# A four-layer graph attention stack on one core: attention logits computed by matmuls of their own, ahead of the values, and the third layer's sums copied out by ScalarE and scaled on GpSimd

## The chip, the cores and the metric

The kernel runs on one core of a Trainium2 chip. Its time is the device time of one execution in microseconds (us). The kernel before was run three times: 3017.86, 3018.09 and 3025.92 us, median 3018.09. The engines are named as in the profile: PE is TensorE (PEld its weight loads), ACT is ScalarE, DVE is VectorE, POOL is GpSimd, SP is SyncE, which issues most DMAs.

## The reference

There are 16 graphs of 1024 nodes with 256 features, and an adjacency matrix for each. Four attention layers follow each other; each normalises x, applies relu, attends, and adds the result to x. Layers 0, 1 and 2 have four heads of 64 columns, layer 3 has one head of 256. In layers 0 and 1 it is, cut to what matters:

```python
h = jnp.maximum(_layernorm(x, axis=-1), 0.0)
v = (h @ W).reshape(B, N, H, HD)                      # values
s = einsum('bnhd,hd->bhn', v, a1); d = einsum('bmhd,hd->bhm', v, a2)   # logits' two halves
e = leaky_relu(s[:, :, :, None] + d[:, :, None, :], 0.2)
e = where(adj == 0, -inf, e)
x = x + einsum('bhnm,bhmd->bhnd', softmax(e), v)
```

Layer 3 is the same with one head. Layer 2 has one pair of vectors for each edge type and, after the attention, adds a bias, takes relu, adds v, and normalises each head's 64 columns with gamma and beta. As adj holds only 0 and 1, only the first edge type occurs in the fast path that is measured here.

So s and d are vectors, one number for each node and head, and linear in h: they can be had as h times (W a), without v.

## The kernel before, in words

Nodes of a graph lie in 8 blocks of 128. A *unit* is one layer of one graph, so there are 64. For a unit with four heads there are 32 *tiles*, one for each head h and source block j; a tile is 128 x 1024 numerators. A tile passes three engines: `weigh` (ACT, lines 991 to 996) makes r = relu(scale * row + bias) in one of two PSUM buffers r; `cover` (DVE, line 1009) adds a constant, multiplies with the mask and writes p to one of 13 buffers in SBUF; `gather` (PE, line 1075) issues 16 matmuls of 65 columns that add p times the values, and the sum of p in column 65, into one of two PSUM banks `po`. This works without a maximum per row because the exponential of a leaky relu splits into products of factors `fac` that depend on one node only, and into a row, kept as `rows`, that depends on the other. All tiles of layers 0 to 2 together are 16 x 3 x 32 = 1536. Layer 3 has work of its own, `last_layer` and `last_sums` (lines 1178 and 1193), which is fitted in between.

What goes before a unit is `prepare` (line 801): bn_stats on DVE, nine small operations `rs` on POOL, and then for each of four *pairs* of blocks: two normalised blocks `hn` on POOL, four transposes on PE, relu to `hT` (`normal`, line 750), and for each block of the pair `project` (line 777): four matmuls of the turned block with the weights `wa`. The weights of each head have two further columns, W times the two attention vectors, made once at the start by `weights` (line 640). So one projection gives, per head, 64 values, s and d: 4 x 66 = 264 columns, in layer 3 258, copied from PSUM to `v`. When all eight blocks are there, DVE takes the maximum of s and d (`wide`, line 861), PE and DVE turn and spread it, DVE and ACT make the factors, and the row goes through DRAM into `rows`. `others` (line 890) makes the remaining factors, and then either POOL multiplies the values by a factor (`flatten`, layers 0 and 1) or writes 1 into the values' column for the sum (layers 2 and 3).

What comes after a tile's sums is `evacuate` (line 1108): in layers 0 and 1 a copy of the PSUM bank to `att`, in layer 2 on DVE a reciprocal of the sums and a multiply. `finish` (line 1128) then works on both halves of a head: in layers 0 and 1 a reciprocal on DVE and a multiply on POOL, in layer 2 the bias and normalisation, and at last the addition to x, all mostly on POOL. For the last two heads of the last unit of the tiles, `main[-1]`, DVE does what POOL does elsewhere.

The order on every engine is fixed when the program is built. A planner (`Plan`, line 417) keeps a clock for each engine with costs (`cost`, line 437) and picks, again and again, the job that can begin first; among jobs that can begin within `NEAR` = 60 ns of the first it takes the one with the earliest due time (`until`). Every engine then runs its list in order. Units of two graphs alternate (`LANES` = 2). Copies marked `EITHER` may go to ACT or DVE; with `DVE_MORE` = 1e9 they go to ACT. There are two PSUM banks `pp` for everything else than r and po (`BANKS` = 2), and three `hT` buffers (`PAIRS` = 3): a pair's buffer is free when all that read it have been issued. All engine operations are issued through one helper, so that nearly every line of the profile shows L487, and tiles are told apart by their names.

## Time and profile before

| | |
|---|---|
| median of three runs | 3018.09 us |
| profiled execution, its own time | 3014.36 us |
| its span, first to last instruction | 3012.4 us |
| granted TensorE clock, mean | 0.976 |
| busy: PE, PEld, DVE, ACT, POOL | 2694.6, 2262.8, 2650.3, 2414.9, 1571.0 us |
| instructions | 130240 |

The rows of the profile name an operation by its output and inputs, its shape and its number; the page gives, for each, the busy time, the mean of one, and the idle time of the engine just before it. The busy time of an engine is the union of its operations, and an operation's duration can reach into the next one's. The waits are listed as "who waited for whom: us in total, times, longest". A matmul in the code is two instructions in the profile, each with a weight load of its own.

### The profile page before, as it was taken

The numbers are of one execution on the slowest core, as the hardware profiler recorded it, in microseconds if no ns is written. First come the engines' busy times: TensorE is split into PE (matmuls) and PEld (weight loads), VectorE is DVE, ScalarE is ACT, GpSimd is POOL, SyncE is SP. The second block draws the span as 40 slices with busy tenths as digits, with TensorE's granted clock in tenths as the row PEclk, the third lists the DMA queues.
The fourth block names the chain that finished last, engine by engine and source line by source line (L and its number), as shares of the span: only waits on it lengthen the run. The fifth ranks groups of instructions, "written<-read, shape, count | busy, mean of one in ns | idle before, by whom it ended". The sixth has DMA issues, their size and how long they took to land.

```text
span 3012.4 us, 130240 instructions
## 1 busy us (share of the span) xinstructions
PE 2694.6 (89%) x58915; PEld 2262.8 (75%) x58915; DVE 2650.3 (88%) x4065; ACT 2414.9 (80%) x3201; POOL 1571.0 (52%) x2263
## 2 busy tenths in 40 slices
PE   5888889999998989999898998989989899999867
PEld 4777777787776778778787786878778778887745
DVE  5889899899978989898998989989898998999963
ACT  5898888888878788888879788897888879878641
POOL 3445682754736447375463745637375464463630
PEclk8999999999999999999999999999999999999978
DMA  7323211323122131413113141321413213111100
GB/s 139 73 59 73 64 36 55 70 65 83 52 52 74 64 68 55 90 44 82 52 63 76 38 96 38 78 59 61 83 42 80 57 62 73 49 48 49 39 12 28
DMA packets 144292, 186.91 MB, mean 62 GB/s; under 512 B 80760, under 2 KB 116336, under 8 KB 142704
## 3 DMA queue, kind: packets, MB, share of 16 engines
q1 hardware_dynamic: 141680, 161.71, 18.5%
q0 software_dynamic: 2048, 16.78, 5.7%
q8 instruction: 464, 7.60, 1.0%
q14 instruction: 100, 0.82, 0.1%
HBM read 194.38 MB, written 34.40 MB: 76 GB/s over the span
## 4 chain that ended last, share of the span: by engine, by line
PE 35%; DVE 29%; ACT 21%; POOL 7%; issue 5%; DMA 1%; SPq 0%; ACTq 0%; POOLq 0%; DVEq 0%
DVE p L487 19%; PE pp L487 19%; PE po L487 16%; ACT r L487 15%; DVE st L487 3%; POOL att L487 2%; ACT seen L487 2%; DVE att L487 2%; ACT att L487 1%; DVE s L487 1%; DVE c L487 1%; POOL rs L487 1%; POOL hn L487 1%; ACT v L487 1%; ACT hT L487 1%
## 5 line engine op out<-in xcount | busy, mean ns | idle before, releaser
L487 ACT ACTIVATE r<-rows,fac 128x1024 f32<-128x1024 f32 (+1 forms) x1552 | 1766.0, 1148 | 363.3 <-DVE p L487 339.3
L487 PEld LDWEIGHTS po<-v,p 128*64 128x64 f32 x49216 | 1598.1, 140 | 332.4 <-DVE p L487 150.6
L487 PE MATMUL po<-v,p 128*64 128x65 f32 x49216 | 1665.0, 225 | 202.0 <-DVE p L487 128.7
L487 DVE SCALAR_TENSOR_TENSOR p<-r,mask 128x1024 f32<-128x1024 f32 x1024 | 1220.5, 1217 | 112.2 <-ACT r L487 86.8
L487 DVE SCALAR_TENSOR_TENSOR p<-r,fac,mask 128x1024 f32<-128x1024 f32 (+1 forms) x768 | 817.9, 1098 | 88.3 <-ACT r L487 71.0
L487 PE MATMUL pp<-wa,hT 128*64 128x264 f32 (+1 forms) x4056 | 518.3, 391 | 13.6 <-ACT hT L487 10.2
L487 POOL TENSOR_TENSOR att<-att,inv 128x512 f32<-128x512 f32 x128 | 133.9, 1046 | 744.6 <-DVE inv L487 628.3
L487 PE MATMUL pp<-v_one,p 128*64 128x257 f32 x3584 | 430.7, 383 | 2.7 <-DVE p L487 1.8
L487 PEld LDWEIGHTS pp<-wa,hT 128*64 128x64 f32 x4056 | 269.3, 138 | 138.9 <-ACT hT L487 16.5
L487 PEld LDWEIGHTS pp<-v_one,p 128*64 128x64 f32 x3584 | 267.2, 138 | 95.2 <-DVE p L487 9.0
L487 POOL TENSOR_SCALAR hn<-x_cur,rs 128x256 f32<-128x256 f32 x512 | 281.6, 562 | 36.4 <-PE pp L487 22.3
L487 PE MATMUL pp<-ident,hn 128*128 128x128 f32 x1020 | 178.8, 295 | 63.5 <-POOL hn L487 51.8
L487 POOL TENSOR_TENSOR x_cur<-att,x_cur 128x512 f32<-128x512 f32 x190 | 226.3, 1191 | 14.9
L487 ACT ACTIVATE r<-rows_one,fac 128x512 f32<-128x512 f32 x240 | 183.4, 778 | 19.3 <-DVE p L487 9.9
L487 PEld LDWEIGHTS pp<-ident,hn 128*128 128x128 f32 x1020 | 108.4, 143 | 120.3 <-POOL hn L487 91.9
L487 DVE BATCH_NORM_STATS2 st<-x_cur 128x6 f32<-128x256 f32 x512 | 180.8, 410 | 11.9 <-DMA x_cur<-in_x_dram 10.2
L487 ACT ACTIVATE hT<-pp 128x512 f32<-128x512 f32 x255 | 147.7, 594 | 39.3 <-PE pp L487 37.9
L487 ACT COPY v<-pp 128x264 f32<-128x264 f32 (+1 forms) x395 | 146.3, 383 | 21.1 <-PE pp L487 18.9
L487 POOL TENSOR_TENSOR v<-v,fac 128x512 f32<-128x512 f32 x128 | 136.1, 1088 | 47.3 <-ACT fac L487 47.3
L487 POOL TENSOR_TENSOR att<-att,s 128x512 f32<-128x512 f32 x124 | 133.1, 1074 | 10.0
L487 ACT ACTIVATE seen<-mask 128x1024 bf16<-128x1024 fp8e4 x128 | 134.6, 1052 | 0.4
L487 POOL TENSOR_TENSOR rs<-st 128x8 f32<-128x8 f32 x192 | 37.9, 211 | 153.9 <-DVE st L487 138.8
(91 smaller groups left out, 1616.3 us busy)
## 6 DMA issues: line engine op xcount, KB each, us to landing
rows<-line SPq DMA_DIRECT2D x191, 512.0 KB
x_cur<-in_x_dram SPq DMA_DIRECT2D x32, 512.0 KB
near<-in_adj_dram POOLq DMA_DIRECT2D x64, 256.0 KB, 8.1
out_dram<-y SPq DMA_DIRECT2D x128, 128.0 KB
rows_one<-line SPq DMA_DIRECT2D x15, 512.0 KB
mask<-near SPq DMA_TRANSPOSE x64
wa<-in_L_gnn_W_dram SPq DMA_DIRECT2D x6, 128.0 KB
line<-row SPq DMA_DIRECT2D x48, 16.0 KB
```

Of the source, the lines that this page charges most:

```text
L487: r = call(*a, **k)
```

## The change

It does four things.

1. Logits. A new job `logits` for each pair of blocks: eight matmuls of the turned blocks with the two further columns of all heads (8 columns, in layer 3 two), into a `pp` bank, and one copy to a new small tile `sd`. `project` now leaves these columns out: 256 columns instead of 264 or 258, and rows of `v` have 65 columns for each head instead of 66. `prepare` goes on to the maximum as soon as `sd` is complete. A pair's `hT` buffer is now read by three jobs.
2. Due times. Logits take the due time that projections had; projections are due `BEHIND` = 20 tiles later.
3. Values. `flatten`, or the writing of ones, waits for the values itself; `fac` loses an unused quarter, and its numbering moves by one; `st`, `rs` and `c` have three buffers instead of two. The planner's cost of a matmul with at most 16 output columns is 30 ns.
4. Evacuation. In layer 2, all units but the last of the tiles are treated as layers 0 and 1 are: a copy of the sums by ACT, then a reciprocal for the head on DVE and the multiply on POOL in `finish`.

```diff
+BEHIND = 20
...
-            return swap + max(59.0, size(out) * 0.833 + 3.0), PE_LATE
+            return swap + (30.0 if size(out) <= 16 else max(59.0, size(out) * 0.833 + 3.0)), PE_LATE
...
+        add(u.until, logits(e), plan.now)
         for i in range(2):
-            add(u.until, project(e, i), plan.now)
+            add(u.until + BEHIND, project(e, i), plan.now)
+
+    def logits(e):
+
+        u = e.u
+        yield "PE", lambda: u.layer in folded and free_for(u) and max(folded[u.layer], free_for(u))
+        pd, left = bank_for(u)
+        pd = pd[:, : 2 * 2 * u.n].rearrange("p (i h c) -> p i h c", i=2, c=2)
+        for i in range(2):
+            for k in range(KC):
+                for c in range(0, P, P // 2):
+                    at = i * P + c
+                    pe.matmul(
+                        pd[c : c + P // 2, i],
+                        e.hT[:, k, at : at + P // 2],
+                        wa[u.layer][:, k, :, u.w :],
+                        start=(k == 0 and i == 0),
+                        stop=(k == KC - 1),
+                        skip_group_check=True,
+                    )
+        e.left -= 1
+        e.read = plan.now
+        yield EITHER, None
+        either_copy(u.sd[:, 2 * e.pair : 2 * e.pair + 2], pd)
+        left()
+        u.begun += 2
+        u.known = plan.now
...
-                    wa[u.layer][:, k, :, :].rearrange("p h e -> p (h e)"),
+                    wa[u.layer][:, k, :, : u.w],
...
-        st = small.tile([P, NB, 2, 3], F32, name="st", bufs=2)
+        st = small.tile([P, NB, 2, 3], F32, name="st", bufs=3)
...
-            e.u, e.pair, e.turned, e.left = u, pair, False, 2
+            e.u, e.pair, e.turned, e.left = u, pair, False, 3
...
-        yield "DVE", lambda: not u.left and u.there
-        s, d = (v[:, :, :, w + c].rearrange("p b h -> p h b") for c in range(2))
+        yield "DVE", lambda: u.begun == NB and u.known
+        s, d = (u.sd[:, :, :, c].rearrange("p b h -> p h b") for c in range(2))
...
-            yield "POOL", None
+            act.activation(u.fac[:, 0:2], arg[:, 1:3], AF.Exp)
+            if not u.shared:
+                yield "POOL", None
+                pool.tensor_scalar(u.fac[:, 2], u.fac[:, 1], -1.0, 0.0, ALU.mult, ALU.add)
+            u.ready = plan.now
+            yield "POOL", lambda: not u.left and u.there
...
+    by_copy = lambda u: u is not main[-1]
...
-        yield EITHER if u.shared else "DVE", lambda: finishing[0] < ATTS or (u, h) in taking
+        yield EITHER if by_copy(u) else "DVE", lambda: finishing[0] < ATTS or (u, h) in taking
...
-        if u.shared:
+        if by_copy(u):
             either_copy(att[:, q, :], po)
...
-        if u.shared:
+        if by_copy(u):
             yield "DVE", None
             dve.reciprocal(u.inv[:, h, :], total)
             yield name, None
             eng.tensor_mul(att, att, wide(u.inv[:, h, :]))
```

More of the change, by code (lines that the diff above doesn't have):

```diff
@@ L554, in fast_path @@
     WIDTH = [F // n + 2 for n in HEADS]
-    VW = max(n * w for n, w in zip(HEADS, WIDTH))
+    VW = max(n * (w - 1) for n, w in zip(HEADS, WIDTH))
     MAXN = max(HEADS)
@@ L773, in normal @@
         left()
+        add(u.until, logits(e), plan.now)
         for i in range(2):
-            add(u.until, project(e, i), plan.now)
+            add(u.until + BEHIND, project(e, i), plan.now)
[23 more added lines that the diff above has]
+        u.known = plan.now
     def project(e, i: int):
         u = e.u
-        width = u.n * (u.w + 2)
         yield "PE", lambda: u.layer in folded and free_for(u) and max(folded[u.layer], free_for(u))
         pv, left = bank_for(u)
+        pv = pv[:, :F].rearrange("p (h e) -> p h e", h=u.n)
         for k in range(KC):
@@ L786, in project @@
                 pe.matmul(
-                    pv[c : c + P // 2, :width],
+                    pv[c : c + P // 2, :],
                     e.hT[:, k, at : at + P // 2],
-                    wa[u.layer][:, k, :, :].rearrange("p h e -> p (h e)"),
+                    wa[u.layer][:, k, :, : u.w],
                     start=(k == 0),
@@ L795, in project @@
         yield EITHER, None
-        either_copy(u.v[:, 2 * e.pair + i, :width], pv[:, :width])
+        either_copy(u.v[:, 2 * e.pair + i, : u.n * (u.w + 1)].rearrange("p (h e) -> p h e", h=u.n)[:, :, : u.w], pv)
         left()
@@ L804, in prepare @@
         slope = SLOPE[layer]
-        width = n * (w + 2)
+        width = n * (w + 1)
         yield "DVE", lambda: (
@@ L816, in prepare @@
         v = u.v[:, :, :width].rearrange("p b (h e) -> p b h e", h=n)
+        u.sd = small.tile([P, NB, n, 2], F32, name=f"sd{n}", bufs=3)
         plan.now = max(plan.now, u.g.here)
         xt = u.g.x
-        st = small.tile([P, NB, 2, 3], F32, name="st", bufs=2)
+        st = small.tile([P, NB, 2, 3], F32, name="st", bufs=3)
         for i in range(NB):
@@ L824, in prepare @@
         yield "POOL", None
-        rs = small.tile([P, 6, NB], F32, name="rs", bufs=2)
+        rs = small.tile([P, 6, NB], F32, name="rs", bufs=3)
         m0, m1, q0, q1 = st[:, :, 0, 1], st[:, :, 1, 1], st[:, :, 0, 2], st[:, :, 1, 2]
@@ L860, in prepare @@
         mx = mine[:, 1, : 2 * n].rearrange("p (c h) -> p c h", c=2)
-        dve.tensor_reduce(mx, v[:, :, :, w : w + 2].rearrange("p b h c -> p c h b"), AX.X, ALU.max)
+        dve.tensor_reduce(mx, u.sd.rearrange("p b h c -> p c h b"), AX.X, ALU.max)
         yield "PE", free_bank
@@ L874, in prepare @@
         yield "DVE", None
-        c = small.tile([P, 7, MAXN], F32, name="c", bufs=2)
+        c = small.tile([P, 7, MAXN], F32, name="c", bufs=3)
         S, D, t, c1, c2, b1, b3 = (c[:, i, :n] for i in range(7))
@@ L887, in prepare @@
         dve.scalar_tensor_tensor(arg[:, 0], s, 1.0 - slope, wide(b1), ALU.mult, ALU.add)
-        u.fac = small.tile([P, 4, n, NB], F32, name=f"fac{n}", bufs=3)
+        u.fac = small.tile([P, 3, n, NB], F32, name=f"fac{n}", bufs=3)
         def others():
@@ L901, in others @@
             yield "ACT", None
-            act.activation(u.fac[:, 1:3], arg[:, 1:3], AF.Exp)
-            yield "POOL", None
+            act.activation(u.fac[:, 0:2], arg[:, 1:3], AF.Exp)
[4 more added lines that the diff above has]
+            yield "POOL", lambda: not u.left and u.there
             if u.shared:
@@ L907, in others @@
                 pool.memset(v[:, :, :, w], 1.0)
-                pool.tensor_scalar(u.fac[:, 3], u.fac[:, 2], -1.0, 0.0, ALU.mult, ALU.add)
                 u.flat = plan.now
-            u.ready = plan.now
         add(u.until, others(), plan.now)
@@ L959, in flatten @@
     def flatten(u: "Unit", v: bass.AP):
-        flat = u.fac[:, 2].rearrange("p h b -> p b h")
+        flat = u.fac[:, 1].rearrange("p h b -> p b h")
         for b in range(0, NB, 2):
@@ L993, in weigh @@
         r, k = wide_bank()
-        base = -1.0 if u.shared else u.fac[:, 3, h, j : j + 1]
-        act.activation(r, u.row[h][0], AF.Relu, bias=base, scale=u.fac[:, 1, h, j : j + 1])
+        base = -1.0 if u.shared else u.fac[:, 2, h, j : j + 1]
+        act.activation(r, u.row[h][0], AF.Relu, bias=base, scale=u.fac[:, 0, h, j : j + 1])
         weighed.append((u, None, h, j, r, k, plan.now))
@@ L1004, in weigh_some @@
         for k in range(MANY):
-            scale = u.fac[:, 1, 0, j + k : j + k + 1]
-            act.activation(r[:, k], of, AF.Relu, bias=u.fac[:, 3, 0, j + k : j + k + 1], scale=scale)
+            scale = u.fac[:, 0, 0, j + k : j + k + 1]
+            act.activation(r[:, k], of, AF.Relu, bias=u.fac[:, 2, 0, j + k : j + k + 1], scale=scale)
         weighed.append((u, i, 0, j, r, at, plan.now))
@@ L1013, in cover @@
         if i is None:
-            base = 1.0 if u.shared else u.fac[:, 2, h, j : j + 1]
+            base = 1.0 if u.shared else u.fac[:, 1, h, j : j + 1]
             dve.scalar_tensor_tensor(by_blocks(p), by_blocks(r), base, mask(u.g, j), ALU.add, ALU.mult)
@@ L1021, in cover @@
                 m = mask(u.g, j + c)[:, i]
-                dve.scalar_tensor_tensor(p[:, c], r[:, c], u.fac[:, 2, h, j + c : j + c + 1], m, ALU.add, ALU.mult)
+                dve.scalar_tensor_tensor(p[:, c], r[:, c], u.fac[:, 1, h, j + c : j + c + 1], m, ALU.add, ALU.mult)
                 u.ps.append((p[:, c], k, plan.now))
@@ L1031, in make_whole @@
         whole[0] += 1
-        base = -1.0 if u.shared else u.fac[:, 3, h, j : j + 1]
-        act.activation(p, u.row[h][0], AF.Relu, bias=base, scale=u.fac[:, 1, h, j : j + 1])
+        base = -1.0 if u.shared else u.fac[:, 2, h, j : j + 1]
+        act.activation(p, u.row[h][0], AF.Relu, bias=base, scale=u.fac[:, 0, h, j : j + 1])
         yield "POOL", None
-        pool.tensor_scalar(p, p, 1.0 if u.shared else u.fac[:, 2, h, j : j + 1], 1.0, ALU.add, ALU.mult)
+        pool.tensor_scalar(p, p, 1.0 if u.shared else u.fac[:, 1, h, j : j + 1], 1.0, ALU.add, ALU.mult)
         yield "POOL", None
@@ L1083, in gather @@
         po = g[0]
-        at = h * (w + 2)
+        at = h * (w + 1)
         for q in range(QUAD):
@@ L1130, in finish @@
         n, w = u.n, u.w
-        at = h * (w + 2)
+        at = h * (w + 1)
         wide = lambda ap: ap.unsqueeze(2).to_broadcast([P, NB, w])
@@ L1274, in fast_path @@
             u.g, u.layer, u.n, u.w = g, layer, HEADS[layer], F // HEADS[layer]
-            u.finished, u.row, u.weighed, u.spent, u.left = {}, [], 0, False, NB
+            u.finished, u.row, u.weighed, u.spent, u.left, u.begun = {}, [], 0, False, NB, 0
             u.ps = []
```

## The prediction

> **What bounds the kernel now.** I read the page first (busy time of each engine, then the chain that ended last), then the list of waits cut to the middle of the run, then three stretches of the timeline for the price of single operations.

> ```profile
> PE 2694.6 (89%) x58915; PEld 2262.8 (75%) x58915; DVE 2650.3 (88%) x4065; ACT 2414.9 (80%) x3201; POOL 1571.0 (52%) x2263
> PE 35%; DVE 29%; ACT 21%; POOL 7%; issue 5%; DMA 1%; SPq 0%; ACTq 0%; POOLq 0%; DVEq 0%
> ```

> Two engines are nearly full, a third is close, and the chain changes hands between all three: no single engine is "the" bound. The waits from 75 to 2840 us (start and end left out) say who stops for whom:

> ```profile
> DVE p L487 <- ACT r L487: 152.1, 257, 5.7
> DVE wide L487 <- ACT v L487: 3.1, 8, 0.5
> ACT r L487 <- DVE p L487: 323.5, 438, 5.1
> PE po L487 <- DVE p L487: 107.2, 89, 7.6
> PE pp L487 <- POOL hn L487: 26.1, 30, 1.9
> ```

> ScalarE and VectorE are tied by the two PSUM buffers r; TensorE hangs more loosely behind them by 13 p tiles. The wait that the change goes at, `wide` (the first operation that needs s and d) for the values, is 3.1 us (and 7.7 once for v_one) in the middle. It is large in two places only, 17.0 us at the start and 16.8 us at the end. One graph's stages in the steady part (32 tiles each: layer 2, then two of layers 0 and 1) are these; the columns are the stretch, its length, and busy us of PE, PEld, DVE, ACT, POOL:

> ```profile
> 1457.50:1522.40 64.90, 56.37 (x1214) 45.80 (x1212) 62.66 (x94) 51.71 (x63) 45.01 (x64) 1.00 0.12 40
> 1522.40:1575.00 52.60, 51.63 (x1216) 45.86 (x1214) 48.60 (x73) 40.52 (x50) 29.34 (x37) 1.00 0.21 70
> 1575.00:1637.80 62.80, 57.78 (x1268) 47.65 (x1264) 53.35 (x86) 58.42 (x88) 24.63 (x43) 0.98 0.45 84
> ```

> DVE fills the first stage, PE and DVE the second, ACT (copies of hT and v) the third.

> [...] a matmul of 65 columns lasts 225 ns (mean) while 80 of them take 2.36 us, 29.5 ns each. So PE's 89% holds pipeline tails; counted by spacing I get some 2480 us, level with DVE. [...] That is the point of my forecast, and the trace has it, in the few matmuls of 8 columns:

> ```profile
> 1009.79 2.36 PE po L487 x80
> 135.08 0.44 PEld L487 LDWEIGHTS po<-v,p 128*64 128x64 f32 x12
> 135.43 0.20 PEld L487 LDWEIGHTS pp<-wide,ones 128*64 128x64 f32 x4
> 135.54 0.38 PEld L487 LDWEIGHTS po<-v,p 128*64 128x64 f32 x10
> ```

> Four loads for 8-column matmuls begin at 135.43 and the next kind's at 135.54: about 28 ns each, no faster than the 65-column ones. A short matmul behind a 64-column load costs what a long one costs.

> **The change part by part** (prices are spacings from start to start; a matmul in the code is two instructions).

> PE, added: logits are 8 matmuls for each of 256 pairs, 2048, 4096 instructions. Bounds: 15 ns each [...] (61 us), 29 ns by the row above (119 us). I take 119. PE, removed: 264 to 256 columns in 1536 projections and 258 to 256 in 512; 32 instructions of 257 columns take 3.48 us, 109 ns, 0.42 ns a column, so -11 us. Net **+108 us**.

> DVE, removed: 120 of the 128 evacuations of layer 2 (all but the last unit's), each a reciprocal and a multiply. From the reciprocal at 1477.48 to the next p at 1478.03 is 0.55 us:

> ```profile
> 1477.48 0.17 DVE L487 RECIPROCAL inv<-po 128x4 f32<-128x4 f32 x1
> 1477.68 0.42 DVE L487 TENSOR_TENSOR att<-po,inv 128x256 f32<-128x256 f32 x1
> 1478.03 1.27 DVE L487 SCALAR_TENSOR_TENSOR p<-r,fac,mask 128x1024 f32<-128x1024 f32 x1
> 1585.66 0.64 ACT L487 COPY v_one<-pp 128x258 f32<-128x258 f32 x2
> 1586.19 1.13 ACT L487 ACTIVATE r<-rows,fac 128x1024 f32<-128x1024 f32 x1
> ```

> That is -66 us; 60 reciprocals on att come back at about 0.13 us, +8. Net **-58 us**. Reading s and d from sd rather than from v keeps counts and sizes: nothing.

> ACT: "either" always falls to ACT at this setting, as it does for every such copy now. 120 copies of 260 columns at 0.265 us (the two copies above take 0.53 us before the next r) are +32. 256 copies of sd (16 or 4 columns) have no row: below, 0.265 less 244 columns at 0.83 ns (from hT's 0.49 us for 512 against 0.265 for 258), 0.06; above, the 0.214 us of the 128x16 exponential. I take 0.10, +26 us (15 to 55). 512 value copies are 2 to 8 columns narrower, -3. Net **+55 us**. Each adds to ACT's queue ahead of an r, for which DVE waits.

> POOL: 60 multiplies att by inv at 1.046 us, **+63 us**, 4.2 in a layer-2 stage where POOL is busy 45.0 of 64.9. Behind them stand the next unit's rs and hn, on which PE waits 26.1 us in all now; 0 to 10 us. The values' multiply by fac (or the memset) is now issued only after the last value copy, later than before. PE's first sums of a unit wait for it, but the unit is prepared tens of tiles ahead: nothing, with up to 5 us if that cover is gone.

> Waits and buffers: one more tenant, 256 times, in the two pp banks, each kept for 0.46 us of matmuls plus a place in ACT's queue behind an r (up to 1.14 us). PE stalls in order meanwhile: 0 to 15 us, inside the range. In exchange layer 2's po banks are freed by a 0.38 us copy rather than 0.6 us on DVE; PE waits 19.9 us for that release now and 19.4 us for ACT's. Equal. Deeper st, rs and c remove no wait in the list. SP issues the same 608 DMAs; its order follows the plan, and ACT waited 4.8 us for rows: nothing.

> Order. Projections get a later due time, so one unit's 32 matmuls are spread over 5 to 16 tiles where they stood within 2.5 to 5: less burst. Against the title, the ring of three hT buffers holds the fourth pair until both projections of the first are issued, so not all logits stand in front.

> Start and end. At the end, three value projections and one 16-matmul group of the older graph's sums stand before the last logits, so `wide` begins no sooner than now (13 us after the first transpose); but that group, 3.5 us, leaves the PE-bound tail. With the logits' own 1.9 us each, start and end give about -3 us together.

> **The sum.** Three ways, all on the profiled execution, 3014.36 us with a span of 3012.4:
> - By the chain: an engine's share of the chain over its busy share says how much of a us added there shows. PE 0.35/0.89, DVE 0.29/0.88, ACT 0.21/0.80, POOL 0.07/0.52: 108 x 0.39 - 58 x 0.33 + 55 x 0.26 + 63 x 0.13 = 42 - 19 + 14 + 8 = +45, ends -3: +42.
> - By stages: I counted what each engine has between first and last tile of a stage in the order of both kernels' instructions, times spacings. For ACT, DVE, PE: first stage 49.6, 59.6, 57.7 becomes 47.8, 51.8, 52.3; second 39.6, 46.4, 45.3 becomes 43.9, 48.0, 54.0; third 55.7, 50.3, 51.9 becomes 56.6, 52.6, 55.3. The fullest engines sum to 161.7 before (the three stages took 180.3) and 162.9 after, +1.2 a graph, +19 over 16 graphs, ends -3: +16.
> - If the p ring evens out all stages, the fullest in total counts: DVE's 156.3 a graph before, PE's 161.6 after, +5.3, +85 in all: an upper end.

> I take +36 on the profiled execution, 3050; the median shown is 3.7 us above that execution, so **3052**, 1.1% slower.

> **Rivals.**
> - Faster: DVE stays the pace. For it: 88% busy, PE waits 107 us for p and could take work there. Then -58, of which a third comes back as waits on ACT (+55 in its queue), -38, ends -3: about 2977. It decides if a logit instruction costs 15 ns, not 29 (PE +50 only), and PE's idle time takes the rest. Against: the second stage, where PE goes from 45.3 to 54.0 past DVE's 48.0.
> - PE sets the pace throughout: 3014 + 85 and bank waits, about 3100. For it: PE's total passes DVE's by 5.3 a graph. Against: ACT still fills the third stage, where PE's extra hides.
> - Nothing that can be measured: the relief in layer 2 (59.6 to 52.3) pays for the second stage, the spread saves the rest: 3018.

> **How the numbers follow.** Forecast, 3028 to 3078: 0.48. Faster rival, 2955 to 3008: 0.20. PE throughout, 3078 to 3125: 0.18. Nothing, 3009 to 3027: 0.14. The three times shown spread over 0.27%, so about 0.3%, 9 us, is what a measurement can tell. The cases lie each on one side of it: faster 0.20, within 0.14, slower 0.66. Eight in ten: 2998 to 3092.

> **What would show it.** Logit loads about 28 ns apart, 4096 more PE instructions, PE's busy share over 91% (right); about 15 ns apart (wrong, and with it the forecast). DVE busy about 2595, ACT 2470, POOL 1634. DVE's wait for r up from 152; PE's wait for p down from 107 towards 70. In the steady part the stage after layer 2 longer than 52.6 us (near 60), the layer-2 stage shorter than 64.9 (near 58). `wide` at the end waiting about as long as now. I am wrong if the second stage stays at 53, or if the multiply on POOL delays hn so that PE's 26.1 us wait doubles.

## The result

The changed kernel takes 3029.13 us in the median of 20 runs (3019.81 to 3042.5), the kernel before 3016.96 us in as many runs beside them. The ratio is 1.0038, with a 95% interval of 1.0027 to 1.0049: slower, by 12 us, a third of the 36 us that were forecast. (The forecast's last step, 3050 + 3.7, makes 3054 and not 3052.) The profiled execution has a span of 3027.2 us (3012.4 before).

First the busy times, from the page of the changed kernel. They came as forecast (DVE 2595, ACT 2470, POOL 1634, PE over 91%):

```profile
PE 2786.2 (92%) x63011; PEld 2397.0 (79%) x63011; DVE 2589.2 (86%) x3885; ACT 2471.4 (82%) x3577; POOL 1627.8 (54%) x2323
```

So VectorE lost 61 us of work, ScalarE and GpSimd gained 57 each, and TensorE gained 92. The page's chain covers only the last fifth of this run, and its shares can't be set beside those of before.

The timeline of the changed kernel gives the price of the new operations; the columns are start, time, engine, operation and number:

```profile
1608.89 0.59 PE L488 MATMUL pp<-wa,hT 128*64 128x8 f32 x16
1609.33 0.67 PE L488 MATMUL po<-v,p 128*64 128x65 f32 x16
...
1609.53 0.17 ACT L488 COPY sd<-pp 128x16 f32<-128x16 f32 x1
1609.60 1.12 ACT L488 ACTIVATE r<-rows,fac 128x1024 f32<-128x1024 f32 x1
```

From the first of 16 logit instructions to the next kind it is 0.44 us, 27.4 ns each, which is also the median of all such groups of 16 in the trace, and 4096 of them make 112 us (119 forecast). The `sd` copy holds ScalarE for 0.07 us, not for its 0.17: the next operation begins inside it.

The waits from 75 to 2855 us, start and end left out (r is what `weigh` makes, p the numerators that `cover` makes of it):

```profile
ACT r L488 <- DVE p L488: 197.5, 337, 5.6
DVE p L488 <- ACT r L488: 176.6, 309, 3.4
PE po L488 <- DVE p L488: 60.5, 75, 4.9
DVE inv L488 <- ACT att L488: 30.7, 28, 7.0
DVE wide L488 <- ACT sd L488: 25.1, 10, 5.5
```

ScalarE waits less for VectorE (323.5 before), VectorE more for ScalarE (152.1), TensorE much less for p (107.2). That is a kernel whose slack has moved from TensorE to VectorE. The three stages of one graph in the steady part (stretch, length, busy us of PE, PEld, DVE, ACT, POOL) read

```profile
1473.31:1536.09 62.78, 58.43 (x1342) 49.81 (x1340) 60.24 (x89) 54.70 (x77) 43.38 (x61) 1.00 0.16 53
1536.09:1587.76 51.67, 49.89 (x1133) 43.44 (x1133) 46.89 (x70) 41.93 (x55) 32.38 (x36) 1.00 0.19 57
1587.76:1651.72 63.96, 61.91 (x1471) 53.26 (x1469) 52.17 (x83) 57.36 (x94) 26.49 (x51) 1.00 0.43 84
```

against 64.90, 52.60 and 62.80 us before. In the second and third stage TensorE is now busy for all but 1.8 and 2.1 us. The second did not grow to 60, and the first shrank by 2 us, not by 7. Together the three take 178.4 us where they took 180.3, though the kernel as a whole grew: one graph's stages do not stand for all sixteen.

**A ledger of TensorE.** From here on I use one reading for all kernels: from 75 us to 172 us before the end, how long the stretch is, how long TensorE is busy in it, and what is left. Two of its lines, of the kernel before and of the changed one (the last three columns are the clock, the DMA share and GB/s):

```profile
75.00:2840.00 2765.00, 2527.49 (x56775) 2139.69 (x56772) 2512.66 (x3792) 2312.80 (x3056) 1498.88 (x2141) 0.99 0.25 62
```

```profile
75.00:2855.00 2780.00, 2618.24 (x60674) 2266.09 (x60672) 2455.60 (x3619) 2373.61 (x3429) 1554.13 (x2201) 0.99 0.25 62
```

Before, TensorE was free for 237.5 us of 2765, after for 161.8 of 2780. Its busy time grew by 90.7, its free time fell by 75.7, and the difference is the 15 us by which the stretch grew. The question of the study is therefore why a kernel with so little free time on TensorE took 91 us more work there and grew by 15.

### The profile page after: what moved, and what is told of

It is laid out like the page before. It is cut to its first block, busy times and chain, and to the rows that moved or that the text cites. A ratio compares the mean times of both kernels' runs of the same rounds, so it can differ in the third digit from the quotient of the medians.

```text
span 3027.2 us, 138841 instructions
## 1 busy us (share of the span) xinstructions
PE 2786.2 (92%) x63011; PEld 2397.0 (79%) x63011; DVE 2589.2 (86%) x3885; ACT 2471.4 (82%) x3577; POOL 1627.8 (54%) x2323
## 3 DMA queue, kind: packets, MB, share of 16 engines
q1 hardware_dynamic: 141680, 161.71, 18.2%
q0 software_dynamic: 2048, 16.78, 5.5%
## 5 line engine op out<-in xcount | busy, mean ns | idle before, releaser
L488 PE MATMUL pp<-wa,hT 128*64 128x256 f32 (+2 forms) x8112 | 661.0, 293 | 25.0 <-ACT hT L488 16.7
L488 PEld LDWEIGHTS pp<-wa,hT 128*64 128x64 f32 x8112 | 418.3, 139 | 143.9 <-ACT hT L488 26.5
L488 POOL TENSOR_TENSOR att<-att,inv 128x512 f32<-128x512 f32 x188 | 196.3, 1044 | 600.8 <-DVE inv L488 496.2
L488 PEld LDWEIGHTS pp<-v_one,p 128*64 128x64 f32 x3584 | 273.4, 138 | 93.9 <-issue 7.2
L488 ACT COPY v<-pp 128x256 f32<-128x256 f32 x396 | 146.4, 374 | 82.3 <-PE pp L488 80.7
L488 ACT ACTIVATE r<-rows_one,fac 128x512 f32<-128x512 f32 x240 | 184.0, 780 | 19.6 <-DVE p L488 13.3
L488 ACT COPY att<-po 128x260 f32<-128x260 f32 x376 | 135.2, 375 | 53.0 <-PE po L488 34.5
```

Source lines behind the costliest of these rows:

```text
L488: r = call(*a, **k)
```

## The experiments

Changes of time are the measured ratio, less 1, times 3017 us, so that runs beside different runs of before can be set side by side. The changed kernel is +11.5 in this measure.

### The evacuation alone

```diff
+    by_copy = lambda u: u is not main[-1]
-        yield EITHER if u.shared else "DVE", ...
+        yield EITHER if by_copy(u) else "DVE", ...
-        if u.shared:
+        if by_copy(u):
```

(in the kernel before; the last line twice)

> The kernel before with the evacuation of layer 2 by a ScalarE copy and GpSimd multiply alone; projections still carry s and d. Theory A (TensorE's extra work makes the loss, the evacuation is a gain): DVE busy about 60 us less, PE busy as before, time 10 to 25 us below the kernel before (ratio 0.992 to 0.997). Theory B (the loss comes from the order that the planner makes and from the end of the run, not from TensorE's work): no telling sign, within 0.3% of before or slower. Theory C (the moved copies load ScalarE, which holds up r): slower than before, ratio above 1.003.

Measured: 3003.89 us, ratio 0.9948 (0.9935 to 0.9961), -15.7 us. This part of the change is a gain, and it beats both kernels.

### The logits alone

```diff
-    by_copy = lambda u: u is not main[-1]
+    by_copy = lambda u: u.shared
```

(in the changed kernel: layer 2's sums go back to VectorE)

> The changed kernel with layer 2's evacuation put back on VectorE: the logits, due times and buffers alone. Theory A: slower than the changed kernel, since DVE keeps its 58 us while PE has its 101 us more (112 of logits less 11 of columns): ratio to before 1.008 to 1.014. Theory B: about that of the changed kernel, 1.002 to 1.006. Theory C: faster than the changed kernel, ratio below 1.002.

Measured: 3030.6 us, ratio 1.0044 (1.0031 to 1.0057), +13.3 us. Theory B holds. In the changed kernel's order the evacuation is worth only 13.3 - 11.5 = 1.8 us, within the intervals: the gains of the two parts do not add up.

### The logits without the put-back

```diff
-BEHIND = 20
+BEHIND = 0
```

> The changed kernel with BEHIND at 0: projections due when logits are. PE work is the same. Theory A: time within 0.5% of the changed kernel, 1.000 to 1.009 of before. Theory B (the order decides): over 0.5% away from the changed kernel, and the projections' bursts come back, so slower, 1.009 or more.

Measured: 3091.81 us, ratio 1.0235 (1.0215 to 1.0255), +70.9 us. One constant of the order, which adds no work, is worth 59 us. The prediction had given it no price.

### The logits twice

```diff
+        for i in range(2):            # all eight once more, behind the first eight
+            for k in range(KC):
+                for c in range(0, P, P // 2):
+                    at = i * P + c
+                    nc.tensor.matmul(pd[c : c + P // 2, i], ...)
         e.left -= 1
```

(not told to the planner, so the order stays)

> The changed kernel with each logits matmul issued a second time, not told to the planner, so that the order of all other instructions stays: PE gets about 112 us more (4096 instructions of 27.4 ns), nothing else. This prices TensorE time by itself. Theory A: by TensorE's share of the chain, 0.39 of it shows: +44 us on the changed kernel, ratio to before about 1.018 (1.010 to 1.030). Theory B: TensorE's work lies in its slack behind the ring of p tiles: less than +12 us, ratio 1.004 to 1.008.

Measured: 3157.61 us, ratio 1.0444 (1.0417 to 1.0471), 122 us above the changed kernel for 112 us of TensorE work. That is 1.1 us for each us; I had priced it at 0.39.

### The same load, half as much up and down

```diff
+        for i in range(2):            # k == 0 only: four of the eight once more, ahead of the eight
+            for k in range(1):
+                for c in range(0, P, P // 2):
+                    at = i * P + c
+                    nc.tensor.matmul(pd[c : c + P // 2, i], ...)
         for i in range(2):
```

```diff
                     at = i * P + c
+                    if k:
+                        plan.spend("PE", 30.0, PE_LATE)
+                        continue
                     pe.matmul(
```

> The changed kernel, its order kept, with half of the logit matmuls issued once more: +56 us of TensorE work, half of what the run with all of them twice had (that one cost some 125 us). A kink at the changed kernel (slack used up just there): +56 to +65 us, about 3090, ratio 1.023. A smooth rise of the price: +35 to +50 us, 3065 to 3080. A cost per instruction that is constant above and below: +62.

> The changed kernel, its order kept, with the second half of the contraction of the logits left out (s and d are then half sums): 1024 fewer short matmuls, -56 us of TensorE work. A kink at the changed kernel: -8 to -25 us, 3005 to 3021. Price above 1 on both sides (TensorE sets the pace already and the order of the changed kernel pays the rest): -56 to -65 us, about 2968. Constant 0.39: -22, 3007.

Measured: with half of them once more 3080.16 us, ratio 1.0204 (1.0181 to 1.0226); with half of them left out 2985.26 us, ratio 0.9884 (0.986 to 0.9908). In the order of the changed kernel, 56 us of TensorE work are worth 46.5 us below it, 50.0 above it, and 72.5 from there to the logits twice. There is no kink at the changed kernel. The price of a us is 0.83, 0.89, 1.29: high on both sides. Some 18 of the last 72.5 us are TensorE's clock, by the estimate that is explained under the ledger (41 us lost with the logits twice, 23 with half of them once more); so that the price itself rises is not shown.

### The load in the order of before

```diff
         for k in range(KC):
             for c in range(0, P, P // 2):
                 at = i * P + c
+                nc.tensor.matmul(pv[c : c + P // 2, : 2 * u.n], e.hT[:, k, at : at + P // 2],
+                                 wa[u.layer][:, k, :, u.w :], start=(k == 0), stop=(k == KC - 1))
+        for k in range(KC):
+            for c in range(0, P, P // 2):
+                at = i * P + c
                 pe.matmul(
```

(in `project`, which overwrites them; once with the evacuation by copy, once in the kernel before as it is)

> The kernel with the evacuation alone, in its own order, plus the 2048 short logit matmuls as a pure load: four ahead of each value projection, into the same PSUM bank, overwritten by the projection, so no copy, no bank and no place in the order is added. +112 us of TensorE work at 27.4 ns an instruction. Theory A (TensorE has slack, and the logits use it up): close to the changed kernel, 3020 to 3035 us, ratio 1.000 to 1.006 to the kernel before. Theory B (a us of TensorE shows at a constant share of 0.39, as I priced it): 3048, ratio 1.010. Theory C (the changed kernel's order, copies and banks are what costs, not TensorE's work): 3004 to 3012, ratio 0.995 to 0.998. Theory D (TensorE is full, the later projections pay for it in the changed kernel): 3080 to 3120.

> The kernel before in its own order, plus the same 2048 short matmuls as a pure load (+112 us of TensorE work), with VectorE still carrying layer 2's evacuations. Theory A (slack beside VectorE): 3025 to 3040, ratio 1.003 to 1.008. Theory B (constant 0.39): 3062, ratio 1.0145. Theory D (full price): 3120 to 3130, ratio 1.035.

Measured: 3088.72 us, ratio 1.0232 (1.0209 to 1.0254), and 3117.03 us, ratio 1.0330 (1.0303 to 1.0357). The same 2048 matmuls cost 85.7 us on top of the evacuation and 99.6 us on top of the kernel before, 0.77 and 0.89 for each us. So a us of TensorE's work cost nearly a us already before the change. That it alone set the pace is not shown: no run loads VectorE or ScalarE by itself, and the evacuation, which relieves VectorE, is worth more beside the load (99.6 - 70.0 = 29.6 us) than without it (15.7). My first thought after the result, that the logits went into free time, is wrong: as bare work they cost 86 us, and something in the changed kernel gives back about 60.

### What gives it back: put-back, early logits, or both

```diff
-            add(u.until, project(e, i), plan.now)
+            add(u.until + 20, project(e, i), plan.now)
```

(with the evacuation by copy and s and d still inside the projections; once without the load and once with it, all four short matmuls ahead of a block's own)

> The kernel with the evacuation alone, and the projections put back by 20 steps as in the changed kernel, but with s and d still inside them: no logit matmuls. It asks whether the later projections are worth something without the early logits. Ledger of TensorE between 75 us and 172 us before the end: the changed kernel with the projections not put back stands idle 199 us and loses 64 us to half clock; the changed kernel 160 and 28. Theory A (the spread alone fills TensorE's idle time and keeps its clock): up to 75 us below the evacuation alone, 2930 to 2965 us, ratio 0.971 to 0.982. Theory B (with s and d inside, the unit's first operation waits for the last projection, and what the spread saves is lost there): 2990 to 3040, ratio 0.990 to 1.007. Theory C (the spread only undoes a crowding that the logits themselves make): as the evacuation alone, 3000 to 3010, ratio 0.994 to 0.997.

> The kernel with the evacuation alone, the projections put back by 20 steps with s and d still inside them, and the 2048 short matmuls added as a pure load. It is the missing corner: without the early logits, the put-back was worth 8 us without the load (3004 to 2996); with the early logits and the load it was worth 63 (3092 to 3029). Theory A (the put-back is worth so much only because TensorE is fuller with the load in it): 3025 to 3045, ratio 1.002 to 1.009. Theory B (it needs s and d to be had early, so that the put-back projections hold nobody): 3075 to 3095, ratio 1.019 to 1.026, 85 us above the run with the put-back alone.

Measured: 2995.54 us, ratio 0.9932 (0.9916 to 0.9948), and 3079.53 us, ratio 1.0213 (1.0193 to 1.0233). With the evacuation by copy in all of them, the runs make this table (us against the kernel before):

| | projections not put back | put back by 20 |
|---|---|---|
| no logit matmuls | -15.7 | -20.5 |
| logit matmuls as a bare load | +70.0 | +64.3 |
| logit matmuls that give s and d early | +70.9 | +11.5 |

Down the first two rows the load costs 85.7 and 84.8. Along them the put-back is worth 5 to 6 us, load or not, which is within the intervals. Early logits alone are worth nothing (70.0 to 70.9, which takes in their copies, the narrower projections and the deeper buffers). Both together are worth 58.5. So it is neither TensorE's fuller queue nor the put-back alone: in these runs late projections pay only when s and d no longer come out of them.

Two runs give the same steps with layer 2's sums still on VectorE: the bare load takes +99.6, early logits put back +13.3, so there they give back 86.3 us. The gain of the order and the relief of VectorE replace each other: the evacuation is worth 15.7 us in the order of before, 29.6 there with the load, and 1.8 in the new order. Each of these kernels has a plan of its own, and a plan can be a few us better or worse for no reason that the table names (one changed cost moves the time by 9 us below); 58.5 and 86.3 stand well clear of that.

### Other settings of the order

```diff
-BEHIND = 20
+BEHIND = 40
```

```diff
-BEHIND = 20
+BEHIND = 10
```

```diff
-            return swap + (30.0 if size(out) <= 16 else ...), PE_LATE
+            return swap + (55.0 if size(out) <= 16 else ...), PE_LATE
```

> The changed kernel with the projections put back by 40 steps in place of 20. Theory A (spread pays for the logits and its gain is not used up): 2990 to 3020, ratio 0.991 to 1.001. Theory B (the projections have no more time to spread into, since hT's ring of three and the next unit hold them): within 0.3% of the changed kernel, 3020 to 3038. A loss, 3045 to 3090, if values now come late for the first sums.

> The changed kernel with the projections put back by 10 steps. If the spread's gain grows evenly from 0 to 20 steps: halfway between 3092 and 3029, 3055 to 3065, ratio 1.011 to 1.015. If it is had at once: 3025 to 3040. TensorE's idle time and its time at half clock should lie between those of the runs with 0 and 20 steps (199 and 160 us idle; 157 and 61 us at half clock).

> The changed kernel with the order's own price of a short logit matmul at 55 ns, as measured (two instructions of 27.4 ns), in place of 30: the order alone changes. If the underpriced logits leave TensorE's bursts misplaced: 10 to 25 us faster, 3004 to 3019, ratio 0.995 to 1.000. If not: within 0.4% of the changed kernel, 3017 to 3041.

Measured: 3252.31 us, ratio 1.0779 (1.0764 to 1.0793); 3037.2 us, ratio 1.0069 (1.0051 to 1.0087); 3035.89 us, ratio 1.0069 (1.0054 to 1.0083). Most of the gain of the put-back is there at 10, with 174.2 us free on TensorE and 106 us at half clock, both between those of 0 and 20 steps in the ledger below, as expected; at 40 it turns into a loss of 235 us against the kernel before, far beyond what I expected. TensorE's waits in that run, from 75 to 3072 us, show what it stands for:

```profile
PE pp L488 <- POOL hn L488: 80.5, 32, 26.2
...
PE pp L488 <- ACT v L488: 43.8, 48, 5.2
PE po L488 <- POOL v L488: 29.1, 5, 15.8
```

Values and normalised blocks now come late (15.6 us for hn in the changed kernel, and no line for v among its costliest). That the ring of three hT buffers carries this, as an unissued projection holds its pair's buffer, fits the lines but was not isolated. The planner's true price for a logit matmul gains nothing; it costs 9 us against the changed kernel, with intervals apart, by a change of order alone.

### The ledger of the runs

Window, busy and free us of TensorE as above; in the last column the time for which the trace records half clock in the same stretch.

| kernel | window | PE busy | free | half clock |
|---|---|---|---|---|
| before | 2765 | 2527.5 | 237.5 | 72 |
| evacuation alone | 2755 | 2534.4 | 220.6 | 106 |
| the same, put back | 2750 | 2535.3 | 214.7 | 109 |
| before and load | 2869 | 2653.6 | 215.4 | 116 |
| evacuation and load | 2840 | 2635.8 | 204.2 | 109 |
| the same, put back | 2828 | 2625.7 | 202.3 | 89 |
| logits, not put back | 2853 | 2652.4 | 200.6 | 157 |
| the changed kernel | 2780 | 2618.2 | 161.8 | 61 |
| put back by 40 | 2997 | 2696.5 | 300.5 | 300 |

The bare load's 112 us took only 22 us out of TensorE's free time in the order of before, and 16 beside the evacuation: in a fixed order most of the free time stayed where it was.

From the evacuation with the load to the changed kernel the stretch is 60 us shorter: 42 us of free time, and 18 us of busy time, of which some 14 are the clock by an estimate (TensorE's busy time within the half-clock time, halved: 42 us lost against 28; in the traces of the kernel before and of the changed one, 65-column matmuls stand 54.2 ns apart at half clock and 29.2 at full, which makes the lost share 0.46). From the logits without put-back it is 73 us: 39 free, and 34 busy; the profiled execution of that kernel is the slowest of its five, 10 us above their median, so that 73 stands for a measured 59. TensorE's costliest waits in these three runs, first the evacuation with the load (75 to 2915 us), then the logits without put-back (75 to 2928 us), then the changed kernel:

```profile
PE po L487 <- DVE p L487: 99.1, 85, 8.1
...
PE pp L487 <- ACT hT L487: 11.9, 10, 6.4
PE pp L786 <- ACT hT L487: 6.8, 16, 1.4
```

```profile
PE po L488 <- DVE p L488: 60.2, 80, 4.4
PE pp L488 <- ACT hT L488: 40.9, 45, 2.8
...
PE pp L488 <- ACT sd L488: 18.5, 6, 3.8
```

```profile
PE po L488 <- DVE p L488: 60.5, 75, 4.9
...
PE pp L488 <- ACT hT L488: 18.2, 22, 1.9
...
PE pp L488 <- ACT sd L488: 1.1, 2, 0.9
```

Early logits take 39 us off the wait for p. Without the put-back 22 of these come back as waits for hT, the turned blocks (18.7 with the load, where the short matmuls stand at L786, and 40.9 here), and 18.5 come as waits for `sd`; half clock is at its longest of all runs but the put-back by 40. With the put-back both waits go (18.2, and 1.1 for sd). The likely reason is that without it the projections stand right behind the transposes and logits of their own pair, and with it other work stands between. This is how the traces read side by side; no run changed one of these waits alone. Why early logits shorten the wait for p is open: that the factors of a unit are ready sooner and leave the planner more to choose from would fit, and was not tested. What the early, put-back order would be worth without the load could not be tried, as it needs the logit matmuls; with half of them left out, which leaves s and d incomplete, it stood at -35.0 us.

## Why the prediction was off

The direction was right: added TensorE work outweighs VectorE's relief. The size was three times too large, and two terms of the sum were wrong against each other, which brought the sum nearer by luck.

- **TensorE's price (the term 108 x 0.39 = +42).** The instructions were right (112 us measured for 119). The price from the chain's share was not: the runs with the load alone give 0.77 and 0.89, +86 to +100 us, and the changed order 0.83 to 1.29. The prediction also set PE's busy share aside and counted 2480 us by spacing; neither this nor the 237.5 us that were free of 2765 gave the price, since the load took only 16 to 22 us of the free time.
- **Order: the step that failed.** The prediction said "Projections get a later due time, so one unit's 32 matmuls are spread over 5 to 16 tiles where they stood within 2.5 to 5: less burst", and gave it no us. With the early logits it is worth -58.5 where the evacuation is by copy, and -86.3 where it is not. It is by far the largest gain of the change. I had argued that readying a unit earlier is worth nothing because it is prepared tens of tiles ahead, and had looked for the gain of the early s and d only where `wide` waits. It shows as TensorE's free time and clock.
- **Evacuation (-19 for DVE, +8 for ACT's copies, +8 for POOL, together -3).** Alone it is -15.7, beside the bare load -29.6, in the changed order -1.8. Its worth depends on the order, which shares of one chain can't tell.
- **The sum.** As measured: evacuation -15.7, load +85.7, early and put back -58.5, which is +11.5; taken in another sequence (load +99.6, early and put back -86.3, evacuation -1.8) it is the same sum of other terms. The stage count, +16, came nearest, but not for its reason: the second stage was to last 60 us and lasts 51.7, which was the prediction's own sign of being wrong, and the first was to last 58 and lasts 62.8. That the order shifts TensorE's work between stages, by way of the 13 p tiles, would fit and was not isolated.
- **ScalarE (+55 forecast).** Busy +56.5. VectorE's waits for r rose from 152.1 to 176.6, and for the copies of `att` from 9.4 to 30.7, so part of VectorE's relief came back as waits, as forecast. The `sd` copies hold ScalarE for some 15 us where the next operation follows at once (0.05 to 0.07 each), at my lower bound; the 0.83 ns a column in its working is 0.89 by the two copies named there.
- **GpSimd.** The multiply did not delay hn: TensorE's wait for it fell from 26.1 to 15.6 us.
- **A logit's price.** The price taken for a short matmul, that of a long one, nearly held: in the changed kernel's trace a logit instruction takes 27.4 ns (29 forecast), and one of 65 columns 29.2 ns, both medians at full clock. The 15 ns of the lower bound was my own assumption, which no trace shows. With half clock recorded from 2927.19 to 2944.26, the 32 logit instructions of the first line take 54 ns each up to the next start:

```profile
2939.33 1.88 PE L488 MATMUL pp<-wa,hT 128*64 128x2 f32 x32
2941.06 5.24 PE L488 MATMUL pp<-v,p 128*64 128x257 f32 x32
```

- **Ends (-3 forecast).** No gain shows. The changed kernel's last preparation, TensorE's first transposes and VectorE's `wide`:

```profile
2935.10 2.30 PE L488 MATMUL pp<-ident,hn 128*128 128x128 f32 x8 [10.29 <-POOL hn L488]
...
2951.38 0.17 DVE L488 TENSOR_REDUCE wide<-sd 128x2 f32<-128x16 f32 x1 [4.35 <-ACT sd L488]
```

It is 16.3 us from one to the other, 13.2 before (2922.66 to 2935.82). The prediction had them equal. In the changed kernel the fourth pair's transposes come after the first pair's projections, as it said, and these stand behind 32 instructions of sums. That this is what costs 3 us is not shown: the evacuation alone, without logits, takes 16.2 us for the same steps (2909.77 to 2926.00).

- **Rivals.** "PE sets the pace throughout" priced the load nearest (+85) and was furthest from the time, as it too left out the order. "Faster" is true of the evacuation alone.

**A better kernel.** The evacuation by copy without the logits takes 3003.89 us, with the projections put back 2995.54; both beat both kernels. Their intervals overlap, so that the put-back's own 5 us are a gain is not shown.

## What to carry to other kernels

Price added work on an engine by a dummy load in an unchanged order, where it can be run: here the engine's share of the chain was too low by half, and its free time, twice the load, took up hardly a fifth of it. When an edit also changes a due time, measure the order by itself, with the edit and without it: here it was worth 5 us alone and 58 with its partner. Gains of parts taken from different engines do not add: the relief of VectorE was worth 16 us alone, 30 with TensorE's load in the old order, and 2 with the same load in the new order.

## What the hardware showed that I had not expected

By the estimate of the ledger, 36 of the 73 us between the logits with and without the put-back are TensorE's clock (64 us lost against 28). Stretches of 10 us of the run without it, with TensorE's busy time in the second column behind the length, and the clock third from the end:

```profile
1490.00:1500.00 10.00, 9.03 (x299) 8.76 (x297) 10.00 (x20) 7.10 (x9) 5.55 (x14) 1.00 0.77 135
1500.00:1510.00 10.00, 5.07 (x72) 3.69 (x69) 9.97 (x18) 9.64 (x15) 7.69 (x12) 0.85 0.01 2
1510.00:1520.00 10.00, 10.00 (x146) 7.30 (x142) 5.77 (x7) 7.97 (x16) 9.01 (x16) 0.80 0.01 2
1520.00:1530.00 10.00, 10.00 (x239) 9.24 (x239) 7.90 (x11) 9.76 (x17) 7.11 (x9) 1.00 0.01 3
```

TensorE is half idle in the second line, and the clock is down at the end of it and in the third, where TensorE is busy throughout. (The 146 instructions there, and 239 in the fourth line, are not the same mix, so they don't measure the clock.) What half clock costs shows in runs of 65-column matmuls in the traces of the kernel before and of the changed one: 54.2 ns from start to start in the median of each, against 29.2 at full clock.
